# A fused attention and feed-forward block: the second entry's rows and the first splits turned by VectorE and HBM instead of TensorE

## The chip, the cores and the metric

The kernel runs on one core of a Trainium2 chip, in one launch. The time is device microseconds of one execution; lower is better. Five engines run side by side, each with its own queue in order: TensorE (PE, with its weight loads PEld), VectorE (DVE), ScalarE (ACT), GpSimd (POOL) and SyncE (SP), which issues all DMAs here. In the profile "L403" is line 403 of the kernel.

## The reference

Two entries of 1024 rows, 512 wide, in float32. Each layer is `x + layernorm(f(layernorm(x)))`: first causal attention with 16 heads of 128, then a gated feed-forward part whose weights are made ternary.

```python
x = x + _layernorm(_L0_attn_ref(_layernorm(x, axis=-1), W_Q, W_K, W_V, W_O), axis=-1)
x = x + _layernorm(_L0_ffn_ref(_layernorm(x, axis=-1), w1, w3, w2), axis=-1)

# attention, for each entry b and head h
q, k, v = (einsum('bsd,hed->bhse', x, W) for W in (W_Q, W_K, W_V))
scores = where(causal, -1e9, einsum('bhse,bhme->bhsm', q, k) / sqrt(128))
out = einsum('bhse,hde->bsd', einsum('bhsm,bhme->bhse', softmax(scores), v), W_O)

# feed-forward, 1365 hidden units; each w made ternary: clip(round(w / s), -1, 1) * s, s = mean(|w|)
out = einsum('bsh,dh->bsd', silu(x @ w1q.T) * (x @ w3q.T), w2q)
```

## The kernel before, in words

**Precision.** The products of the attention part take each float32 operand as three forms in fp32r: a leading one, a low one and their difference (`lead`, `low`, `diff`). The feed-forward part takes the rows as two (`hi`, `lo`), since ternary weights are exact.

**Rows as operands.** A projection needs the normalised rows turned, with the 512 columns on the partitions. One tile is 128 rows by 512 columns. For the first layer `block_unit(b, t)` turns tile t (0 to 7) of entry b: four TensorE transposes of 128x128 into PSUM, then ScalarE writes `lead`, VectorE `low`, GpSimd (or VectorE at the start) `diff`. The turned forms stand in tiles `xb`, of which there are six. For the second layer `split_units` gives three stages: `load` (the rows back from HBM, for entry 0), `normal`, and `split_turn` (four TensorE transposes, then `hi` and `lo`). Only the first split, of entry 0's first four tiles, runs that way. The twelve later ones, in the feed-forward stage, run through `split_stages`: VectorE transposes the tile in blocks of 32x32 (`xs`), one DMA writes it to HBM (`hopx`), four DMAs read it back with the blocks in place (`xu`), and then `hi` and `lo` are made from SBUF.

**Steps.** The attention stage is a loop over 32 (entry, head) pairs n and 8 query tiles i, 256 steps of some 4 to 7 us; `idx` counts them. In each step the source issues, in this order: weight loads; the step's `fill` (projections, output units, values), each on TensorE behind the newest matmul; forms of weights; the scores of three steps ahead (`look(idx + AHEAD)`); the rest of the values; the turning of the probabilities of two steps ahead (`turn`, which writes `blocks` to `hop` and later reads it back as `pt`); and last the step's `side` work. `tc.issue_after` (through `past` and `behind`) sets the order on an engine: the side work stands behind the last row maximum on VectorE, behind the last clearing of `blocks` on GpSimd, and behind the last turn on VectorE or SP. Within these bounds the compiler orders by its own plan. Loads, row statistics and the ternary weights are side work.

**The second entry's rows.** Its first projection stands in step 120. `block_at` is step 117. Tile t is loaded in the side work of step 114 + t, normalised by ScalarE (`normal_unit`, L388) in that of 115 + t, and turned in the fill of step 117 + t (`block_unit`, L403 to L409), with a PSUM buffer of the tag "mm" that the matmuls use as well. `split_at` is step 245: loads three steps ahead, normalisations two ahead (L123), turns in the fill of 245 + t (L256 to L259).

**Buffers.** PSUM holds four buffers "mm" and two "s_ps" for scores. In SBUF, `xt` has three buffers, `zf` (a copy of the values, read by VectorE's low form L667) two, `ones` is a constant for summing over partitions (L165).

**Start.** `busy(k)` issues k transposes of the identity that nobody reads. The first four tiles of entry 0 are turned in the buffers "s_ps".

Of the kernel before, what the change touches and what calls it, by code (L numbers as in the profile page):

```python
# [9 lines left out]
FP = mybir.dt.float32  # L10
# [9 lines left out]
FR = mybir.dt.float32r  # L20
T12 = 4096.0
LEAD = 1.0 - 0.5 / T12
# [13 lines left out]
def sandwich_kernel(  # L36
# [40 lines left out]
    )  # L77
    ones = const.tile([P, P], FP, name="ones")
    nc.gpsimd.memset(ones, 1.0)
    eps = const.tile([P, 1], FP, name="eps")  # L80
# [58 lines left out]
    def mean_abs_units(k, pool):  # L139
        todo = pieces(k)  # L140
        part = keep.tile([P, len(todo)], FP, name=f"part{k}")

        raws = {}

        def load(n):
            src, rows, cols = todo[n]
            raws[n] = raw = pool.tile([P, D], FP, name="xt")
            nc.sync.dma_start(raw[:rows, :cols], src)

        def reduce(n):  # L150
# [12 lines left out]
        def last():  # L163
            ps = ps_m.tile([P, 512], FP, name="tr", tag="mm")
            newest[0] = nc.tensor.matmul(  # L165
                ps[:, 0:1], lhsT=ones, rhs=raws["tot"], start=True, stop=True
            )
            for i, f in enumerate((0.5, -0.5, 1.0)):
                nc.vector.tensor_scalar(
                    scales[k][:, i : i + 1], ps[:, 0:1], 1.0 / (D * F), f,  # L170
                    ALU.mult, ALU.mult,
                )

        pairs = [
            (lambda n=n: load(n), lambda n=n: reduce(n)) for n in range(len(todo))
        ]
        return pairs, total, last
# [51 lines left out]
    def split_units(b, tb, t, stage):  # L229
# [13 lines left out]

        return load, normal, lambda: split_turn(b, tb, t, held["x"])

    def split_unit(b, tb, t, stage):
        for unit in split_units(b, tb, t, stage):
            unit()

    def split_turn(b, tb, t, xt):  # L250
        if t == 0:
            split[b, tb] = [xblocks.tile([P, NC, TB], FR, name="xb") for _ in range(2)]
        bl = split[b, tb]
        ps = ps_m.tile([P, NC, P], FP, name="trx", tag="mm")
        for c in range(NC):
            newest[0] = nc.tensor.transpose(ps[:, c, :], xt[:, ts(c, P)], ident)  # L256
        hi, lo = (part[:, :, ts(t, P)] for part in bl)
        nc.scalar.copy(hi, ps)
        nc.vector.tensor_tensor(lo, ps, hi, ALU.subtract)  # L259

# [77 lines left out]
    with ExitStack() as att:  # L338
# [39 lines left out]
        def block_load(b, t):  # L378
            normal[b, t] = xt = xpool.tile([P, D], FP, name="xt")
            nc.sync.dma_start(xt, x[b, ts(t, P), :])  # L380

        def normal_unit(b, t):
            if b == 0:
# [9 lines left out]
        def block_unit(b, t):  # L393
# [3 lines left out]
            xt = normal[b, t]  # L397
            if b == 0:
                ps = ps_s.tile([P, NC, P], FP, name="tr", tag="s_ps")
            else:  # L400
                ps = ps_m.tile([P, NC, P], FP, name="tr", tag="mm")
            for c in range(NC):
# [234 lines left out]
        def values(n, m):  # L637
# [21 lines left out]
            lead, low, diff = (w[:, ts(half, KB)] for w in zs[g, qb, j])  # L659
            copy = zpool.tile([P, KB], FP, name="zf", bufs=2)  # L660
            for to, scale in ((lead, LEAD / T12), (copy, 1.0)):
# [46 lines left out]
        with past(*done):  # L708
# [3 lines left out]
            for t in range(QT):  # L712
                blocks.append(block_unit(0, t))
                if t % 2 == 1:
                    busy((8, 3)[t // 2])
        lead, low, diff = blocks[-1]
# [32 lines left out]
        block_at = 2 * (NP - 1) * NT + 5  # L749
        assert at + 1 < block_at - 3  # L750
        for t in range(NT):
            side[block_at - 3 + t].append(lambda t=t: block_load(1, t))
            side[block_at - 2 + t].append(lambda t=t: normal_unit(1, t))
        at += (1 - at) % 4 + 4
# [16 lines left out]

        split_at = (N - 2) * NT + 5
        splits = [split_units(0, 0, t, xpool) for t in range(QT)]
        for t in range(QT):
            side[split_at - 3 + t].append(splits[t][0])
            side[split_at - 2 + t].append(splits[t][1])

# [35 lines left out]
        for n in range(N):  # L813
# [22 lines left out]
            if j == 0 and g > 0:  # L836
                outs = output_units(g - 1)
                put((0, 0, 0, 1, 4, 5, 6, 7), outs)
            for t in range(NT):
                if divmod(block_at + t, NT)[0] == n:  # L840
                    put([(block_at + t) % NT], [lambda t=t: block_unit(1, t)])
            for t in range(QT):
                if divmod(split_at + t, NT)[0] == n:
                    put([(split_at + t) % NT], splits[t][2:])
            if n == N - 1:
# [57 lines left out]
    with ExitStack() as ffn:  # L903
# [85 lines left out]

        def split_stages(b, tb, t):  # L990

            load, normal, _ = split_units(b, tb, t, xpool)
            if t == 0:
                split[b, tb] = [xblocks.tile([P, NC, TB], FR, name="xb") for _ in range(2)]
            held = {}

            def turn():
                xs = xpool.tile([P, 4, NC, 32], FP, name="xs", bufs=2)
                nc.vector.transpose(
                    xs.rearrange("p to c r -> p c to r"),  # L1000
                    normal().rearrange("p (b r) -> p b r", r=32),
                )
                held["d"] = d = dram.tile([P, 4, NC, 32], FP, name="hopx", bufs=2)
                nc.sync.dma_start(d, xs)

            def read():
                held["u"] = u = xpool.tile([P, 4, NC, 32], FP, name="xu", bufs=2)
                for to in range(4):
                    nc.sync.dma_start(
                        u[ts(to, 32)].rearrange("x a c r -> x a (c r)"),  # L1010
                        held["d"][:, to].rearrange("(a x) c r -> x a (c r)", a=4),
                    )

            def forms():
                u = held["u"]
                hi, lo = (
                    part[:, :, ts(t, P)].rearrange("p c (a r) -> p a c r", a=4)
                    for part in split[b, tb]
                )
                nc.scalar.copy(hi, u)  # L1020
                nc.vector.tensor_tensor(lo, u, hi, ALU.subtract)

            return load, turn, read, forms

        last = {}
# [91 lines left out]
```

## Time and profile before

| what | value |
|---|---|
| median of 3 runs | 1511.98 us (1511.87 to 1513.71) |
| profiled execution | 1511.27 us |
| its span | 1509.5 us |
| mean granted TensorE clock | 0.997 |
| TensorE transposes of the second entry's rows (L403, xt) | 32, from 592.2 to 627.9 us |
| TensorE transposes of the first splits (L256) | 16, from 1218.2 to 1229.4 us |
| VectorE transposes of the later splits (L999) | 12, median 711 ns |
| landing of hopx<-xs, of xu<-hopx | 2.1 us, 2.1 us (medians) |

The profile gives, for each engine, its busy time and the idle time before each group of instructions, with the instruction whose end released it ("<-DVE acc L530"). The profiled execution is one run; its span leaves out what comes before the first and after the last instruction. Matmuls overlap in the records: the time that one takes from TensorE is the distance to the next one's start. A group of the page with "+7 forms" mixes shapes.

### The profile page before, as it was taken

To read this page: it belongs to the slowest core of one execution; us is meant where nothing else is said; L and a number is where in the kernel's file an instruction comes from. 1 tells how busy PE (TensorE), PEld (TensorE's weight loads), DVE (VectorE), ACT (ScalarE), POOL (GpSimd) and SP (SyncE) were. 2 spreads that over 40 slices of the span, in tenths; PEclk is the share of its full clock that TensorE was granted. 3 is DMA by queue.
4 is the path that set the end of the run, shared out by engine and by line. 5 is a ranking of instruction groups with operands and counts; after the bars stand their busy time and mean duration, and the time that the engine had idled before them with its cause. 6 is when DMAs were issued, how large, how long until landed. Compare 5 with 4: busy or idle time off the path is not lost.

```text
span 1509.5 us, 21335 instructions
## 1 busy us (share of the span) xinstructions
PE 1475.6 (98%) x7061; PEld 1184.9 (78%) x7061; DVE 1080.6 (72%) x2123; ACT 792.7 (53%) x1566; POOL 404.3 (27%) x472
## 2 busy tenths in 40 slices
PE   8999999999999999999999999999999999999997
PEld 6778888887878787777778787878787877888885
DVE  7767686878786878787777777777777776664444
ACT  4656555555555555666664555555555464444332
POOL 3222222222223333434433333333322110210010
PEclk9999999999999999999999999999999999999999
DMA  3666767676666675758866666666665677530200
GB/s 123 194 194 186 195 184 200 185 202 184 201 191 172 181 206 183 205 166 249 238 200 190 195 192 196 195 195 189 179 179 166 181 216 228 176 102 19 91 28 29
DMA packets 179894, 263.57 MB, mean 175 GB/s; under 512 B 19188, under 2 KB 120564, under 8 KB 175688
## 3 DMA queue, kind: packets, MB, share of 16 engines
q1 hardware_dynamic: 179784, 262.20, 59.5%
q8 instruction: 57, 0.93, 0.3%
q14 instruction: 53, 0.43, 0.1%
HBM read 160.43 MB, written 101.71 MB: 174 GB/s over the span
## 4 chain that ended last, share of the span: by engine, by line
PE 66%; issue 10%; DVE 9%; DMA 7%; ACT 5%; POOL 2%; SPq 1%; DVEq 0%; POOLq 0%; ACTq 0%
PE mm L650 11%; PE mm L471 10%; PE mm L318 10%; PE s_ps L556 10%; PE mm L499 8%; PE mm L519 6%; PE yp L933 5%; PE mm L478 5%; DVE nm L565 3%; DMA hop<-blocks 2%; ACT p_sb L572 2%; DMA wqk<-wk 2%; ACT p_sb L578 1%; POOL kl L440 1%; DVE blocks L604 1%
## 5 line engine op out<-in xcount | busy, mean ns | idle before, releaser
L572 ACT ACTIVATE p_sb<-s_ps,nm 128x128 f32<-128x128 f32 (+7 forms) x256 | 190.0, 742 | 367.3 <-DVE nm L565 360.8
L556 PE MATMUL s_ps<-k,q 128*128 128x512 f32 (+3 forms) x768 | 289.7, 486 | 0.7 <-ACT p_sb L572 0.7
L650 PE MATMUL mm<-pt,v_sb 128*128 128x256 f32 (+1 forms) x1280 | 271.7, 359 | 11.3 <-ACT q L454 3.7
L650 PEld LDWEIGHTS mm<-pt,v_sb 128*128 128x128 f32 x1280 | 238.1, 190 | 48.8 <-ACT q L454 6.2
L578 ACT ACTIVATE p_sb<-p_sb,ri 128x128 f32<-128x128 f32 (+7 forms) x256 | 197.7, 773 | 33.0 <-DVE ri L577 30.5
L565 DVE TENSOR_REDUCE nm<-s_ps 128x1 f32<-128x128 f32 (+7 forms) x256 | 193.7, 757 | 7.1
L604 DVE STREAM_TRANSPOSE blocks<-p_sb 128x128 f32<-128x128 f32 (+7 forms) x256 | 197.1, 770 | 1.2 <-ACT p_sb L578 0.9
L556 PEld LDWEIGHTS s_ps<-k,q 128*128 128x128 f32 x768 | 132.3, 190 | 69.4 <-issue 61.4
L670 POOL TENSOR_TENSOR zd<-za,zl 128x256 fp32r<-128x256 f32 x128 | 94.7, 739 | 328.0 <-DVE zl L667 319.7
L561 DVE TENSOR_TENSOR s_ps<-s_ps,causal 128x128 f32<-128x128 f32 x256 | 75.4, 295 | 136.1 <-PE s_ps L556 135.6
L499 PE MATMUL mm<-va,xb 128*128 128x256 f32 x512 | 158.5, 310 | 0.0
L499 PE MATMUL mm<-vd,xb 128*128 128x256 f32 x512 | 144.9, 283 | 0.9 <-POOL xb L409 0.9
L499 PE MATMUL mm<-vl,xb 128*128 128x256 f32 x512 | 144.6, 282 | 0.0
L471 PE MATMUL mm<-xb,qa 128*128 128x512 f32 x256 | 119.6, 467 | 1.0 <-ACT xb L407 1.0
L471 PE MATMUL mm<-xb,ka 128*128 128x512 f32 x256 | 112.3, 439 | 0.0
L499 PEld LDWEIGHTS mm<-vl,xb 128*128 128x128 f32 x512 | 97.7, 191 | 7.1 <-issue 4.1
L499 PEld LDWEIGHTS mm<-va,xb 128*128 128x128 f32 x512 | 97.7, 191 | 7.1 <-issue 3.9
L471 PE MATMUL mm<-xb,ql 128*128 128x512 f32 x256 | 101.7, 397 | 0.0
L471 PE MATMUL mm<-xb,kl 128*128 128x512 f32 x256 | 100.7, 393 | 0.1
L499 PEld LDWEIGHTS mm<-vd,xb 128*128 128x128 f32 x512 | 97.7, 191 | 1.1 <-POOL xb L409 1.1
L601 POOL MEMSET blocks<- 128x128 f32 x128 | 26.2, 205 | 263.1 <-DMA hop<-blocks 185.2
L533 DVE TENSOR_TENSOR acc<-acc,mm 128x512 f32<-128x512 f32 x128 | 86.1, 683 | 12.7 <-ACT acc L528 5.4
(162 smaller groups left out, 2777.3 us busy)
## 6 DMA issues: line engine op xcount, KB each, us to landing
hop<-blocks SPq DMA_DIRECT2D x32, 1024.0 KB, 4.5
pt<-hop SPq DMA_DIRECT2D x128, 256.0 KB, 6.2
hop<-blocks SPq DMA_DIRECT2D x32, 768.0 KB, 3.3
pt<-hop SPq DMA_DIRECT2D x128, 192.0 KB, 3.8
hop<-blocks SPq DMA_DIRECT2D x32, 512.0 KB, 3.2
pt<-hop SPq DMA_DIRECT2D x128, 128.0 KB, 3.2
wqk<-wq SPq DMA_DIRECT2D x32, 256.0 KB, 5.2
wqk<-wk SPq DMA_DIRECT2D x32, 256.0 KB, 6.6
```

The costliest lines, as they stand in the source:

```text
L318: newest[0] = nc.tensor.matmul(ps[:fl, :], lhsT=t[:, c, :], rhs=bl[k][:, c, :], start=(c == 0 and k == 0), stop=(c == NC - 1 and k == 1),)
L471: newest[0] = nc.tensor.matmul(main, lhsT=forms[f][0][:, c, :], rhs=forms[f][1][:, c, :], start=(c == 0 and f == 0), stop=(c == NC - 1 and ...
L499: newest[0] = nc.tensor.matmul((main, main, diff)[f][:, ts(t, 2 * P)], lhsT=forms[f][0][:, c, token], rhs=forms[f][1][:, c, :], start=(t = ...
L519: newest[0] = nc.tensor.matmul((main, main, diff)[f], lhsT=zs[g, t // QT, j][f][:, ts(t % QT, P)], rhs=weights[3, g][f][:, 2 * j : 2 * j + ...
L533: nc.vector.tensor_tensor(dst, dst, diff, ALU.subtract)
L556: newest[0] = nc.tensor.matmul(s_ps[:, ds(k0, kl)], lhsT=proj[n, 0, i // QT][:, ts(i % QT, P)], rhs=proj[n, 1, k0 // TB][:, :kl], start=Tr ...
L565: top = nc.vector.tensor_reduce(nm, s_ps[:, :L], axis=AX.X, op=ALU.max, negate=True)
L572: e = nc.scalar.activation(p_sb[:, :L], s_ps[:, :L], AF.Exp, bias=nm, accum_out=rs)
L578: nc.scalar.mul(p_sb[:, :L], p_sb[:, :L], ri)
L604: turned = nc.vector.transpose(b[:, :, 0 : i + 1, il, :].rearrange("p to t r -> p t to r"), p_sb[:, :L].rearrange("p (b r) -> p b r", r=32),)
L650: newest[0] = nc.tensor.matmul(dst, lhsT=proj[g, 2][:, kt, ts(j, P)], rhs=rhs, start=(kt == 0), stop=(kt == 2 * m + 1),)
L670: nc.gpsimd.tensor_tensor(diff, lead, low, ALU.subtract)
```

## The change

The eight tiles of the second entry and the four of the first split are turned as the later splits are. `turn_stages` holds the two stages `turn` and `read`; `split_stages` moves out of the feed-forward part and uses it, with one buffer for `xs` there as well (two before), and two for `xu`. `block_stages(t)` gives five stages for tile t of the second entry, in the side work 6 (load), 5 (normalise), 4 (turn and write), 3 (read back) and 1 (forms) steps ahead of `block_at + t`. The low form of these is made by four VectorE instructions, one for each 128 columns. The first splits run 5 (load), 4 (normalise, turn and write), 3 (read back) and 1 (forms) steps ahead of `split_at + t`. To find room in SBUF, `zf` goes from two buffers to one, and the constant `ones` becomes a tile of the rotating `xt` that GpSimd sets when it is needed, three times. At the start, tiles 2 and 3 of entry 0 take buffers "mm" in place of "s_ps", and the unread transposes go from 8 and 3 to 7 and 8.

```diff
-    ones = const.tile([P, P], FP, name="ones")
-    nc.gpsimd.memset(ones, 1.0)
...
             ps = ps_m.tile([P, 512], FP, name="tr", tag="mm")
+            ones = pool.tile([P, D], FP, name="xt")
+            nc.gpsimd.memset(ones, 1.0)
             newest[0] = nc.tensor.matmul(
-                ps[:, 0:1], lhsT=ones, rhs=raws["tot"], start=True, stop=True
+                ps[:, 0:1], lhsT=ones[:, :P], rhs=raws["tot"], start=True, stop=True
             )
...
-    def split_turn(b, tb, t, xt):
-        if t == 0:
-            split[b, tb] = [xblocks.tile([P, NC, TB], FR, name="xb") for _ in range(2)]
-        bl = split[b, tb]
-        ps = ps_m.tile([P, NC, P], FP, name="trx", tag="mm")
-        for c in range(NC):
-            newest[0] = nc.tensor.transpose(ps[:, c, :], xt[:, ts(c, P)], ident)
-        hi, lo = (part[:, :, ts(t, P)] for part in bl)
-        nc.scalar.copy(hi, ps)
-        nc.vector.tensor_tensor(lo, ps, hi, ALU.subtract)
+    def turn_stages(pool):
+        held = {}
+
+        def turn(xt):
+            xs = pool.tile([P, 4, NC, 32], FP, name="xs", bufs=1)
+            nc.vector.transpose(
+                xs.rearrange("p to c x -> p c to x"), xt.rearrange("p (b r) -> p b r", r=32)
+            )
+            held["d"] = d = dram.tile([P, 4, NC, 32], FP, name="hopx", bufs=2)
+            nc.sync.dma_start(d, xs)
+
+        def read():
+            held["u"] = u = pool.tile([P, 4, NC, 32], FP, name="xu", bufs=2)
+            for to in range(4):
+                nc.sync.dma_start(
+                    u[ts(to, 32)].rearrange("r a c x -> r a (c x)"),
+                    held["d"][:, to].rearrange("(a r) c x -> r a (c x)", a=4),
+                )
+
+        return turn, read, held
+
+    def by_group(form, t):
+        return form[:, :, ts(t, P)].rearrange("p c (a x) -> p a c x", a=4)
+
+    def split_stages(b, tb, t, pool):
+        load, normal = split_units(b, tb, t, pool)
+        turn, read, held = turn_stages(pool)
+
+        def forms():
+            if t == 0:
+                split[b, tb] = [xblocks.tile([P, NC, TB], FR, name="xb") for _ in range(2)]
+            hi, lo = (by_group(part, t) for part in split[b, tb])
+            nc.scalar.copy(hi, held["u"])
+            nc.vector.tensor_tensor(lo, held["u"], hi, ALU.subtract)
+
+        return load, lambda: turn(normal()), read, forms
...
+        def block_stages(t):
+            turn, read, held = turn_stages(xpool)
+
+            def forms():
+                k, tl = divmod(t, QT)
+                if tl == 0:
+                    xs[1, k] = [xblocks.tile([P, NC, TB], FR, name="xb") for _ in range(3)]
+                lead, low, diff = (by_group(form, tl) for form in xs[1, k])
+                nc.scalar.mul(lead, held["u"], LEAD / T12)
+                for c in range(NC):
+                    nc.vector.scalar_tensor_tensor(
+                        low[:, :, c], lead[:, :, c], -T12, held["u"][:, :, c],
+                        ALU.mult, ALU.add,
+                    )
+                lead, low, diff = (form[:, :, ts(tl, P)] for form in xs[1, k])
+                nc.gpsimd.tensor_tensor(diff, lead, low, ALU.subtract)
+
+            return (
+                lambda: block_load(1, t), lambda: normal_unit(1, t),
+                lambda: turn(normal[1, t]), read, forms,
+            )
...
-            if b == 0:
+            if t in (2, 3):
+                ps = ps_m.tile([P, NC, P], FP, name="tr", tag="mm")
+            else:
                 ps = ps_s.tile([P, NC, P], FP, name="tr", tag="s_ps")
-            else:
-                ps = ps_m.tile([P, NC, P], FP, name="tr", tag="mm")
...
-            copy = zpool.tile([P, KB], FP, name="zf", bufs=2)
+            copy = zpool.tile([P, KB], FP, name="zf", bufs=1)
...
-                    busy((8, 3)[t // 2])
+                    busy((7, 8)[t // 2])
...
-        assert at + 1 < block_at - 3
+        assert at + 1 < block_at - 6
         for t in range(NT):
-            side[block_at - 3 + t].append(lambda t=t: block_load(1, t))
-            side[block_at - 2 + t].append(lambda t=t: normal_unit(1, t))
+            for stage, ahead in zip(block_stages(t), (6, 5, 4, 3, 1)):
+                side[block_at - ahead + t].append(stage)
...
-        splits = [split_units(0, 0, t, xpool) for t in range(QT)]
         for t in range(QT):
-            side[split_at - 3 + t].append(splits[t][0])
-            side[split_at - 2 + t].append(splits[t][1])
+            for stage, ahead in zip(split_stages(0, 0, t, xpool), (5, 4, 3, 1)):
+                side[split_at - ahead + t].append(stage)
...
-            for t in range(NT):
-                if divmod(block_at + t, NT)[0] == n:
-                    put([(block_at + t) % NT], [lambda t=t: block_unit(1, t)])
-            for t in range(QT):
-                if divmod(split_at + t, NT)[0] == n:
-                    put([(split_at + t) % NT], splits[t][2:])
...
-                stages = [split_stages(nb, ntb, t) for t in range(QT)]
+                stages = [split_stages(nb, ntb, t, xpool) for t in range(QT)]
```

More of the change, by code (lines that the diff above doesn't have):

```diff
@@ L242, in normal @@
             return held["x"]
[L244 to L248, printed above, removed]
-    def split_turn(b, tb, t, xt):
-        if t == 0:
-            split[b, tb] = [xblocks.tile([P, NC, TB], FR, name="xb") for _ in range(2)]
-        bl = split[b, tb]
-        ps = ps_m.tile([P, NC, P], FP, name="trx", tag="mm")
-        for c in range(NC):
-            newest[0] = nc.tensor.transpose(ps[:, c, :], xt[:, ts(c, P)], ident)
-        hi, lo = (part[:, :, ts(t, P)] for part in bl)
-        nc.scalar.copy(hi, ps)
-        nc.vector.tensor_tensor(lo, ps, hi, ALU.subtract)
+        return load, normal
+    def turn_stages(pool):
[27 more added lines that the diff above has]
+        return load, lambda: turn(normal()), read, forms
     def middle_units(b, pool):
@@ L988, in finish_last @@
                 nc.sync.dma_start(out[b, ts(tt, P), :], y)
[L990 to L1023, printed above, removed]
         last = {}
```

## The prediction

> **What bounds the kernel now.** I read the page first: who is busy, and what the chain of waits consists of.
>
> ```profile
> span 1509.5 us, 21335 instructions
> PE 1475.6 (98%) x7061; PEld 1184.9 (78%) x7061; DVE 1080.6 (72%) x2123; ACT 792.7 (53%) x1566; POOL 404.3 (27%) x472
> ...
> PE 66%; issue 10%; DVE 9%; DMA 7%; ACT 5%; POOL 2%; SPq 1%; DVEq 0%; POOLq 0%; ACTq 0%
> ```
>
> TensorE (PE) lacks work for only 33.9 us of the span, so the first question of any edit is how much TensorE time it removes, and the second is whether another engine then makes TensorE wait. Both are read from TensorE's timeline around the second entry's rows (t is the tile of 128 rows, 0 to 7).
>
> ```profile
> 590.54 1.78 PE L650 MATMUL mm<-pt,v_sb 128*128 128x256 f32 x8 [1.65 <-DVE acc L530]
> 592.16 0.60 PE L403 MATMUL tr<-ident,xt 128*128 128x128 f32 x4
> 592.59 0.39 PE L556 MATMUL s_ps<-k,q 128*128 128x128 f32 x2
> ...
> 609.65 0.39 PE L499 MATMUL mm<-vd,xb 128*128 128x256 f32 x1 [0.92 <-POOL xb L409]
> ...
> 612.38 0.66 PE L403 MATMUL tr<-ident,xt 128*128 128x128 f32 x4 [1.27 <-ACT xt L388]
> ...
> 614.42 0.65 PE L403 MATMUL tr<-ident,xt 128*128 128x128 f32 x4 [0.31 <-ACT xt L388]
> ```
>
> Four transposes show 0.60 us, but matmuls overlap: what counts is start to next start, 592.16 to 592.59, 0.43 us. The brackets are TensorE idle: 2.5 us of it (0.92, 1.27, 0.31) hang on rows or forms that come late, 1.65 on VectorE (DVE). So I asked for the busy time by stretch, each about one step of the schedule (columns: us, then PE, PEld, DVE, ACT, POOL busy, clock, DMA share, GB/s).
>
> ```profile
> 570.20:576.50 6.30, 6.30 (x29) 5.04 (x28) 3.52 (x9) 3.55 (x8) 1.96 (x3) 1.00 0.46 148
> 576.50:580.00 3.50, 3.50 (x16) 2.44 (x15) 3.11 (x8) 2.15 (x4) 3.16 (x4) 1.00 0.68 201
> 580.00:586.00 6.00, 6.00 (x25) 4.25 (x24) 5.73 (x10) 3.74 (x8) 2.70 (x3) 1.00 0.45 133
> 586.00:593.00 7.00, 5.35 (x28) 4.36 (x27) 5.74 (x10) 4.77 (x9) 0.21 (x1) 1.00 0.70 187
> 593.00:598.10 5.10, 5.10 (x26) 4.20 (x26) 4.75 (x10) 2.47 (x7) 2.20 (x2) 1.00 0.31 127
> 598.10:602.90 4.80, 4.80 (x26) 4.02 (x25) 3.38 (x10) 3.02 (x8) 2.81 (x4) 1.00 0.99 309
> 602.90:608.20 5.30, 5.30 (x41) 4.81 (x40) 2.92 (x8) 2.83 (x7) 3.48 (x3) 1.00 1.05 215
> ```
>
> VectorE is nearly full from 576.5 to 598 and has room before and after. The change puts new VectorE work into exactly these steps.
>
> **The change, part by part.** The sum is against the profiled execution, 1511.27 us (its span and 1.8 us around it), which is 0.7 below the median 1511.98; I add that back at the end.
>
> *TensorE transposes go.* Eight tiles at L403 and four at L256, 12 x 0.43 = 5.2 us, in stretches where TensorE is the bound. Their PSUM slots (tag "mm", shared with the matmuls) go too; I count nothing for that.
>
> *Stalls at those transposes go.* The forms are now finished in the side work of the step before the one in which the transposes stood, so the 0.92, 1.27 and 0.31 go: 2.5 us. What is late next is in the ledger below. At the first splits TensorE waits 0.69 us at 1232.04 (ACT p_sb L572, itself behind VectorE). There VectorE is 4.77 busy of 4.80 from 1220.1 to 1224.9; the earlier stages take two normalisations (L123, about 0.5 us each) out of these steps. I take 0.4 us.
>
> *Start.* Tiles 2 and 3 of the first entry get PSUM buffers of their own, so they no longer wait for VectorE to empty the first two.
>
> ```profile
> 8.90 0.81 ACT L388 ACTIVATE acc<-acc,shift,r_in 128x512 f32<-128x512 f32 x1 [0.43 <-DVE shift L371]
> ...
> 10.97 1.25 PE L403 MATMUL tr<-ident,acc 128*128 128x128 f32 x8 [1.83 <-DVE xb L408]
> ...
> 11.67 1.19 ACT L407 ACTIVATE xb<-tr 128x512 fp32r<-128x512 f32 x2 [0.98 <-PE tr L403]
> ```
>
> Rows 2 are normalised at 9.71, so ScalarE (ACT) can go on at 10.7 instead of 11.67, and VectorE's L408 at 11.5 instead of 12.31: 0.8 us earlier. From there the chain is VectorE's and GpSimd's (POOL), the latter not moved: I take 0.7 us, bounds 0 and 2. For the added filler transposes a rule stands against a row. TensorE: Matmul & The Clock Gate, Part 1, of the Trainium skill lets the clock fall to half after an idle window of about 3.4 us; here the longest gap is 1.83 us, so by the rule filler buys nothing. The row says the granted clock was 0.50 from 14 to 16 us after that gap. By the row a closed gap could save up to 2 us of TensorE time; but qd and kd come from VectorE at 17.57 and 19.26, so both give 0 here and the row only sets the far bound.
>
> *VectorE pays.* The nearest row for the new transpose is the same operation in the later stage, 128x512: 0.71 us (L999), and 0.62 from start to next start by L604's 512-wide one (571.73 to 572.35). Twelve of them, 7.4 us. The low form, one L408 of 0.60 start to start, becomes four pieces of 128 columns. No row has them; below, no more than 0.60 in all; above, four of L561's 0.295, 1.2. From L667's 256 columns (581.30 to 581.63, 0.33) I take 0.21 each, 0.85: 0.25 more per tile, 2 us for eight. The total is 9.4 us, more than the 5.2 that TensorE is spared; it is worth doing only where VectorE has room. Tile 0's turn falls into 2.79 us that VectorE spends waiting for POOL kl before 575.86: free. Before L530 at 589.80, which frees the slot that TensorE waits for at 590.54, come then tile 1's turn (0.62 less 0.32 idle), tile 2's and 3's (0.62 each) and tile 0's low form (0.85): 2.4 us, and the 1.65 stall grows to about 4. In the next two steps each gets 0.62 + 0.25 against 0.33 and 1.42 idle: 0.7 us reach TensorE. In the three steps after 603 there are over 2 us idle each: nothing. At the splits the turns fall into steps with 0.7 to 3.7 us idle: nothing.
>
> Here a rule speaks against the change: VectorE: DVE Perf Modes, Rules for kernel authors, says to transpose 128x128 on TensorE where a PSUM destination will do. By engine time it is right here too (0.43 against 0.71 a tile): 12 x 0.28 = 3.3 us slower, 1515.3. But it prices engines, not the bound: in the trace TensorE has no idle to give and VectorE has some, so I follow the trace.
>
> *The trip through HBM.* Per tile one write and four reads, five issues of about 0.43 us on SP's queue (2.1 us), 0.5 MB. SP stands mostly at L615, waiting for VectorE's blocks; its pt<-hop reads are needed about 9 us after landing, which covers 2 us of issue; past that L650 would wait. With xs at one buffer, a turn waits in VectorE's queue for the write of the tile before to land, and behind it stand L561 and L565, which ScalarE's exponentials and then TensorE wait for. Turns are 3.7 to 6.4 us apart (by L604's ends). In the later stage the write lands in 2.1 us, but here it follows hop<-blocks of up to 1 MB (4.5 us). Tile 5 follows tile 4 after 3.7 us: about 2 us of wait, part in the 1.42 idle: I take 0.8, bounds 0 and 4 for all. DMA share is about 1.0 from 598 to 608; loads move out of it, hops move in: 0.3, bounds -1 and 3. GpSimd contention with the low form, now SBUF only: L1021 has a median of 0.684 and a mean of 0.776, and one of 1.78; 8 x 0.1, of which 0.3 reach TensorE.
>
> *Counted at nothing.* ScalarE's normalisation (L388, 0.80 us) moves three steps ahead, its leading form one; both stay one step behind what they wait for, and ScalarE has 1.2 to 3 us idle a step. If a load lands later than a step, ScalarE waits with the exponentials behind it, as it does for 2.0 us in all now. GpSimd's difference form (1.29 us) moves a step ahead with 2 us idle or more in each. zf with one buffer: ScalarE's second copy must wait for VectorE's zl of the product before. Over 127 pairs the zl had ended 1.9 us or more ahead, but once 0.75; cover gone, ScalarE waits with the exponentials behind it, about as long as VectorE is late (2.4 us, once). The ones tile: a GpSimd memset three times, before L165; GpSimd has gaps of 1 to 3 us before each; without them TensorE waits one 1.3 us L440, 0 to 4 us in all. xs at one buffer in the last stage: turns 2.3 us apart at 1290.9 and 1293.2 could collide, covered by stages that run two steps ahead of their use.
>
> **Sum.** Gains 5.2 + 2.5 + 0.4 + 0.7 = 8.8. Costs 2.4 + 0.7 + 0.8 + 0.3 + 0.3 = 4.5. Net -4.3: 1507.0 beside the profiled run, 1507.7 beside the median.
>
> **Rivals.** *VectorE takes it all back.* If the transfer of work lands wholly where VectorE is full, its 9.4 us reach TensorE against gains of 8.8: 1512.6. For: DVE 5.74 busy in a step in which TensorE already waits. Against: half of the turns fall into steps with idle. *The single xs buffer holds VectorE's queue.* Ten turns follow another. If the write lands as the slowest xt<-x does here (8.2 us, in the stretch where DMA share is 1.0) instead of 2.1, each waits about 3 us: 30 us, less 11 idle in these steps and up to 7 that one step of lookahead covers (scores are issued three steps ahead into two buffers), some 12 on TensorE: 1519.5. It decides once these waits add 7.3 us on TensorE beyond my 0.8. For: DMA share 0.99 and 1.05. Against: most writes here land in 3 to 5 us. *It doesn't do what it says:* rows read back too late, so that matmuls wait for xb as at 609.65; two steps (10 us) lie between read and forms, so this is worth 2 us at most, 1509.7, counted with the even case. *All of VectorE's part is hidden:* 1503.2.
>
> **How the numbers follow.** 0.2% is 3.0 us, about what a measurement of this kernel can tell from no change: faster is below 1509.0, slower above 1515.0. The forecast with the hidden case 0.50, VectorE takes it back 0.25, the xs wait and other late transfers 0.25. The likeliest case alone is 1503 to 1510. The range reaches from 1502 (hidden, with 1 us more at the start) to 1518, leaving out the far part of the slow case.
>
> **What would show it.** L403 with xt and L256 gone; the stall near 590 grown to about 4 us and named after VectorE, no stall on xt or xb between 605 and 615; turns of 0.7 us without idle ended by DMA before them; the first L471 about 1 us earlier. Wrong if TensorE's idle between 560 and 640 exceeds 8 us, or VectorE idles on hopx.

## The result, and the profile after

| kernel | median us | runs | profiled execution, span |
|---|---|---|---|
| before | 1512.85 | 1511.87 to 1514.48 (4) | 1511.27, 1509.5 |
| after | 1526.15 | 1525.48 to 1531.38 (4) | 1525.56, 1523.8 |

The changed kernel takes 1.0094 times as long (95% interval 1.0069 to 1.0119; this ratio and the later ones are of means), 13.3 us more by the medians. I had forecast 4.3 us less. The page of the kernel after, the same lines as shown of before:

```profile
span 1523.8 us, 21439 instructions
PE 1479.1 (97%) x7017; PEld 1185.2 (78%) x7017; DVE 1095.8 (72%) x2159; ACT 792.5 (52%) x1566; POOL 404.6 (27%) x474
...
PE 62%; issue 10%; DVE 10%; DMA 8%; ACT 6%; POOL 2%; SPq 1%; DVEq 0%; POOLq 0%; ACTq 0%
```

TensorE has 44 instructions fewer and is nonetheless busy 3.5 us longer, and it lacks work for 44.7 us in place of 33.9. Of VectorE's 15.2 us more, 8.4 are the twelve added turns. To place the loss I number the score tiles by VectorE's masking of each (L561 before, L610 after: 256 of them, 0 to 255) and subtract their starts. The difference is -0.5 us at tile 0, -0.2 from tile 16 to tile 116, then rises to +10.3 by tile 129 (the second entry's rows), stays between 9.5 and 10.8 until tile 252, rises to +15.0 by tile 255 (the first splits), and is +14.3 at the first and at the last down projection (yp). So there are two losses, about 10.5 and 4.2 us, and none in the feed-forward stage.

TensorE's timeline at the rows (start, duration, instruction, in brackets the idle time before it and what ended it):

```profile
590.12 1.78 PE L699 MATMUL mm<-pt,v_sb 128*128 128x256 f32 x8 [1.41 <-ACT q L503]
...
600.52 4.30 PE L699 MATMUL mm<-pt,v_sb 128*128 128x256 f32 x12 [2.22 <-DMA pt<-hop]
...
611.90 0.38 PE L548 MATMUL mm<-va,xb 128*128 128x256 f32 x1 [1.27 <-ACT xb L417]
...
614.83 1.22 PE L548 MATMUL mm<-vd,xb 128*128 128x256 f32 x4 [0.96 <-POOL xb L424]
...
619.00 3.48 PE L699 MATMUL mm<-pt,v_sb 128*128 128x256 f32 x16 [0.97 <-DMA pt<-hop]
...
641.14 2.87 PE L699 MATMUL mm<-pt,v_sb 128*128 128x256 f32 x8 [4.47 <-DMA pt<-hop]
```

The stall near 590 did not grow (1.65 before). What is new is the wait for pt: probabilities that come back late from their own trip, whose code the change does not touch. The stretch table adds what such a wait costs afterwards (columns as in the prediction; the eighth number is the granted clock):

```profile
599.00:600.00 1.00, 0.00 (x0) 0.00 (x0) 1.00 (x4) 0.72 (x3) 0.00 (x0) 1.00 1.18 199
600.00:601.00 1.00, 0.48 (x2) 0.42 (x3) 1.00 (x5) 0.54 (x1) 0.00 (x0) 0.83 0.44 78
601.00:602.00 1.00, 1.00 (x4) 0.82 (x3) 1.00 (x5) 0.46 (x2) 0.42 (x1) 0.50 0.47 176
602.00:603.00 1.00, 1.00 (x4) 0.82 (x3) 0.49 (x3) 0.57 (x2) 0.85 (x1) 0.50 0.99 182
603.00:604.00 1.00, 1.00 (x4) 0.73 (x4) 1.00 (x4) 0.00 (x0) 0.00 (x0) 0.50 1.07 428
```

A gap of 2.22 us is followed by over 3 us at half clock. The means of the stretches 600 to 605, 610 to 615, 615 to 620 and 640 to 645 are 0.66, 0.93, 0.73 and 0.66, against 1.00 in all seven stretches shown of before. Five times the missing shares is 5.1 us at most. The 10.5 us then read: TensorE's idle time between 560 and 660 grew by 7.9 (4.15 to 12.02), the absent transposes are worth 3.4 by the prediction's price (eight tiles at 0.43), and some 6 remain, of which the clock explains 5.1 at most. About 1 us is placed nowhere.

Why pt comes late is seen in SP's queue. First before, then after:

```profile
582.67 0.34 SPq L615 DMA_DIRECT2D hop<-blocks  x1
583.05 1.39 SPq L380 DMA_DIRECT2D xt<-x  x2
586.86 1.75 SPq L631 DMA_DIRECT2D pt<-hop  x4
```

```profile
584.54 0.35 SPq L664 DMA_DIRECT2D hop<-blocks  x1
586.38 1.93 SPq L262 DMA_DIRECT2D xu<-hopx  x4
593.24 0.34 SPq L257 DMA_DIRECT2D hopx<-xs  x1
593.62 0.43 SPq L406 DMA_DIRECT2D xt<-x  x1
594.17 1.81 SPq L680 DMA_DIRECT2D pt<-hop  x4
```

From 588.3 to 593.2 SP stands at the write of hopx, because VectorE's turn of that tile (L253) runs only at 592.51. Behind it stands the read of pt. Its hop was issued at 584.54 and took 4.7 us to land, so the read could have started at about 589.2. It starts at 594.17, 7.3 us later than before: 5.0 by standing behind the write of hopx, the rest because its own hop landed later (586.8 before). TensorE waits for it until 600.52. Yet VectorE itself never waits for the trip; the groups of its turns show no idle ended by a DMA:

```profile
L253 DVE STREAM_TRANSPOSE xs<-xt 128x512 f32<-128x512 f32 x24 | 16.9, 704 | 0.2
```

So my first theory was that SP's single queue costs it: late turns, or simply five more issues per tile. The rivals: VectorE's added work, the bytes, the single buffer of xs, one of the small edits.

### The profile page after: what moved, and what is told of

Read it like the earlier page. It is cut to its first block, busy times and chain, and to the rows that moved or that the text cites. A ratio compares the mean times of both kernels' runs of the same rounds, so it can differ in the third digit from the quotient of the medians.

```text
span 1523.8 us, 21439 instructions
## 1 busy us (share of the span) xinstructions
PE 1479.1 (97%) x7017; PEld 1185.2 (78%) x7017; DVE 1095.8 (72%) x2159; ACT 792.5 (52%) x1566; POOL 404.6 (27%) x474
## 4 chain that ended last, share of the span: by engine, by line
PE 62%; issue 10%; DVE 10%; DMA 8%; ACT 6%; POOL 2%; SPq 1%; DVEq 0%; POOLq 0%; ACTq 0%
PE mm L699 10%; PE mm L344 10%; PE s_ps L605 9%; PE mm L520 9%; PE mm L548 8%; PE mm L568 6%; PE yp L975 5%; PE mm L527 4%; DMA hop<-blocks 3%; DVE nm L614 3%; ACT p_sb L621 3%; DMA wqk<-wk 2%; DMA pt<-hop 1%; POOL kl L489 1%; DVE blocks L653 1%
## 5 line engine op out<-in xcount | busy, mean ns | idle before, releaser
L610 DVE TENSOR_TENSOR s_ps<-s_ps,causal 128x128 f32<-128x128 f32 x256 | 75.4, 295 | 133.7 <-PE s_ps L605 133.1
```

## The experiments

All medians are beside runs of the kernel before on the same chip (1511.9 to 1512.6 in the five groups of runs).

**Which part of the change.** The three kernels put the rows, the splits, or both back on TensorE, exactly as in the diff's removed lines. rows_only keeps the rows' trip, splits_only that of the splits, rest_only neither.

```diff
 # splits_only and rest_only: rows on TensorE
-            for stage, ahead in zip(block_stages(t), (6, 5, 4, 3, 1)):
-                side[block_at - ahead + t].append(stage)
+            side[block_at - 3 + t].append(lambda t=t: block_load(1, t))
+            side[block_at - 2 + t].append(lambda t=t: normal_unit(1, t))
```

> The first splits go back to TensorE; the second entry's eight tiles stay with VectorE and HBM, and so do the edits at the start, to ones, zf and xs. Read from the two traces, the rows cost 10.5 us, the splits with what follows them 4.2, and the start gives 0.2. If these parts are independent, as the theory of SP's queue has it (each trip delays only the hop writes and pt reads near it): 1512.9 + 10.5 - 0.2 = 1523 us. If the last part of the slowdown is one that the rows cause and that only shows at the end, or that the edits to zf and ones cause, the time stays at 1526.

> The second entry's eight tiles go back to TensorE; the first splits stay with VectorE and HBM. Independent parts: 1512.9 + 4.2 - 0.2 = 1517 us. If the splits are only late because the whole schedule is displaced, or if zf and xs with one buffer are to blame, it is another number: 1513 in the first case, above 1520 in the second.

> Rows and splits both go back to TensorE; left are the start (tiles 2 and 3 in ps_m, more filler), ones in an xt slot, zf and xs with one buffer. The theory gives these 0.2 us of gain: 1512.5 to 1512.9. If zf with one buffer or the ones tile were behind part of the loss, it would be slower than before by 2 us or more. My prediction had 0.7 us of gain for the start.

| kernel | median us | ratio to before, interval |
|---|---|---|
| rows_only | 1522.16 | 1.0062 (1.0047 to 1.0077) |
| splits_only | 1516.36 | 1.0028 (1.0020 to 1.0037) |
| rest_only | 1512.27 | 0.9997 (0.9988 to 1.0005) |

The parts add up: 9.9 and 4.1 us on top of rest_only, together 14.0, against 13.9 measured for the whole. The edits to zf, ones, the start and the feed-forward stage are worth nothing measurable, so the start's 0.7 us of my sum is not there either.

**Another queue.** In the attention stage the trip is issued from another engine: all of it from GpSimd (q_pool), only the write from ScalarE (q_act_write), all of it from ScalarE (q_act).

```diff
-            nc.sync.dma_start(d, xs)
+            nc.gpsimd.dma_start(d, xs)   # q_act_write, q_act: nc.scalar
...
-                nc.sync.dma_start(
+                nc.gpsimd.dma_start(     # q_act: nc.scalar; q_act_write: nc.sync
                     u[ts(to, 32)].rearrange("r a c x -> r a (c x)"),
```

> The changed kernel, with the write of hopx and the reads of xu in the attention stage issued from GpSimd's queue in place of SP's; VectorE's work, xs, zf and all bytes are as in the changed kernel. Theory of SP's queue: hop writes and pt reads no longer stand behind a write that waits for a late turn, the waits of TensorE for pt near 600, 619 and 641 (2.2, 1.0 and 4.5 us) and the lowered clock behind them go, as does most of the 4.2 us at the splits: 1510 to 1516 us, unless GpSimd's own forms are held up by the issues. Theory that VectorE's 9.4 us of added work, or one buffer of xs, is the cause: nothing moves, 1524 to 1528. Theory of DMA bandwidth: the same, 1524 to 1528.

> The changed kernel, with only the write of hopx in the attention stage issued from ScalarE's queue; the four reads of xu stay with SP, and hopx stays on the hardware queues. GpSimd's queue gave 1540.7: the waits for pt were gone there, but ScalarE, VectorE and GpSimd then stood at hopx and xu. Theory of SP's queue, in the form that SP stands still at a hopx write whose turn is late: hop writes and pt reads regain their places except for 1.8 us of reads, and the 7.7 us of idle named after pt mostly go: 1515 to 1521. Rival, that the issue time of the five DMAs fills SP: no better than 1524. If ScalarE now stands at the late turn with the exponentials behind it, it is slower than 1526.

> As the run before, with the reads of xu on ScalarE's queue too. SP is then as in the kernel before. If SP's order is all that counts: 1510 to 1516. If ScalarE stands at the landing of hopx (it did so for 22 us with GpSimd's queue, by way of xu), the exponentials wait for it: 1525 or more. Each trip also takes 2.1 us of ScalarE's time.

Measured: 1540.73, 1533.72 and 1534.81 us (ratios 1.0185, 1.0136 and 1.0149, each within 0.0016). All three are slower than the change, against every number of my theory. What came true are the branches in which ScalarE waits in SP's place: over 1526 for q_act_write, 1525 or more for q_act. In q_pool and q_act TensorE no longer waits for pt between 560 and 660, as the theory had it, but the wait came back elsewhere. In q_act_write, where only the write has left SP, 4.9 of the 7.7 us of waiting for pt remain. The waits of q_pool between 560 and 660 (us in total, times, longest), first TensorE's, then ScalarE's:

```profile
PE mm L549 <- POOL xb L425: 9.3, 1, 9.3
PE mm L700 <- ACT q L504: 6.8, 1, 6.8
```

```profile
ACT xb L418 <- DMA xu<-hopx: 21.9, 6, 7.4
```

GpSimd now stands at hopx with its own difference forms behind, and ScalarE at xu with the exponentials behind. q_pool and q_act bear out that pt was late by what stood ahead of it on SP, but none of the three shows a cure.

**VectorE's work or the DMAs, with dummies.** TensorE turns all rows as before (rest_only). dve_extra adds VectorE's eight turns of a constant tile without DMA. dma_extra adds the eight writes and 32 reads without turns. The next three vary dma_extra: tiny DMAs, the same bytes in two DMAs, reads that need not wait for the write.

```diff
+        def extra_turn(t):        # side work at block_at - 4 + t
+            xs_ = xpool.tile([P, 4, NC, 32], FP, name="xs", bufs=1)      # dve_extra
+            nc.vector.transpose(xs_.rearrange(...), dz.rearrange(...))
...
+            nc.sync.dma_start(d, dz.rearrange("p (a c x) -> p a c x", a=4, c=NC))  # dma_extra
+        def extra_read(t):        # side work at block_at - 3 + t
+            for to in range(4): ...                     # dma_extra: as xu<-hopx
```

> TensorE turns all rows, as in the kernel before; VectorE turns a constant tile of 128x512 into xs besides, in the eight steps in which the changed kernel has its turns (ahead 4), and nothing reads it. No DMA is added. It adds 8 x 0.71 us to VectorE and nothing else. Rival of VectorE's load: about 5 us on top of 1512.3, 1517. Theory of SP's queue: SP does not wait for these turns, so only what VectorE hands on directly: 1512.5 to 1514.5 (my prediction's working had 1.9 us for the turns alone).

> TensorE turns all rows, as in the kernel before; the eight writes of hopx and the 32 reads of xu are added from a constant tile in the same steps of the changed kernel, on SP's queue, and nothing reads xu. No VectorE work is added, and no write waits for a turn. It adds 17 us of issue to SP and 4 MB. If issue time or DMA bandwidth alone is the cause: about 10 us on top of 1512.3, 1522. If it is the standing of SP at writes that wait for late turns: 1513 to 1516.

> As dma_extra (five more DMAs per tile on SP's queue, from a constant tile, TensorE turns all rows), but each DMA moves 16 packets of 128 bytes in place of 256 and 64 KB. The number of issues and their places in SP's order are the same, the bytes are gone. dma_extra stood at 1521.8 beside 1512.3. If what costs is the time in which SP issues and the order in its queue: 1518 to 1522. If it is what the DMA engines have to move: 1512 to 1514.

> As dma_extra, with the same bytes in two DMAs per tile: one write of 256 KB and one read of 256 KB in rows of 2 KB, in place of one write and four reads of 512-byte pieces. SP issues 0.9 us per tile in place of 2.1. If issue time costs: 1513 to 1516. If bytes cost: 1518 to 1522. If the 512-byte pieces are what makes the bytes dear, it also falls to 1513 to 1516; issue_tiny then tells the two apart.

> As dma_extra, with the four reads per tile taken from x in place of hopx, in the same pieces of 512 bytes. So no read waits in SP's queue until a write has landed; issues and bytes are the same. If SP's standing at the landing of hopx (3.5 us in the trace of dma_extra between 570 and 650) moves the rest: 1513 to 1516. If not: 1520 to 1522.

| kernel | median us | ratio to before, interval |
|---|---|---|
| dve_extra | 1512.56 | 1.0006 (0.9997 to 1.0014) |
| dma_extra | 1521.76 | 1.0068 (1.0050 to 1.0085) |
| issue_tiny | 1515.08 | 1.0019 (1.0012 to 1.0026) |
| bytes_two | 1514.41 | 1.0011 (1.0002 to 1.0020) |
| dma_nowait | 1523.22 | 1.0068 (1.0053 to 1.0083) |

Eight turns more on VectorE cost nothing that can be measured: that rival falls. The DMAs alone cost 9.6 us, just the size that was looked for, which looked like an answer: not the issues (2.5), not the bytes (1.9), not the wait for the write's landing (dma_nowait is no better), but issues and bytes together. But TensorE's waits in dma_extra between 560 and 660 are others than in the changed kernel:

```profile
PE tr L463 <- ACT xt L448: 9.8, 5, 2.9
```

Here the rows are still loaded three steps ahead, and TensorE waits for their normalisation (L448). ScalarE shows no idle time ended by a load ahead of it, so the delay is in what ScalarE does first; it was not followed further. In the change the rows are loaded six steps ahead and nobody waits for them; it is pt that is late. A dummy whose loss has the right size and another wait proves nothing for the case. Why issues and bytes together cost more than their sum, the four issues or the 512-byte pieces of the reads, stays open.

**The trip inside the change.** So the next four keep rows_only's own turns and forms and vary only the trip. trip_none reads the forms from xs and makes no trip; trip_two makes it in two DMAs in natural layout; trip_tiny issues all five DMAs with 2 KB each; trip_real makes the real trip, back into the buffer that it left from. All have xs with three buffers and no xu for the rows.

```diff
-            xs = pool.tile([P, 4, NC, 32], FP, name="xs", bufs=1)
+            held["u"] = u = pool.tile([P, 4, NC, 32], FP, name="xs", bufs=3)
...
-            held["u"] = u = pool.tile([P, 4, NC, 32], FP, name="xu", bufs=2)
             for to in range(4):     # trip_real; trip_none leaves the DMAs out
```

> As rows_only (1522.2), with the trip left out for the second entry's rows: VectorE turns each tile into xs (three buffers), the forms are taken from xs three steps later, nothing is written to or read from HBM, so the blocks of 32 are not moved between partitions. VectorE's, ScalarE's and GpSimd's work is that of the change. By the sum of my prediction for the rows alone (3.4 of transposes, 2.5 of stalls, less 3.1 of VectorE and 0.3 of GpSimd): 1512.3 - 2.5 = 1509.8. If VectorE's work is free, as dve_extra showed for the turns: 1506.5 to 1508. If VectorE's low form in four pieces or the order of the forms is to blame: 1515 or more.

> As trip_none, with one write of 256 KB to hopx and one read of 256 KB back into the same buffer in rows of 2 KB, in the steps of the changed kernel: the trip's bytes and both of its waits, in two issues in place of five. Left out: the move of blocks between partitions. If bytes alone cost as with the dummies: trip_none + 2 us. If the bytes or the waits for the turns are the main cost: trip_none + 8 or more.

> As trip_none, with one write and four reads of 16 packets of 128 bytes each on SP's queue; the write waits for VectorE's turn as in the changed kernel, the reads for the write's landing. All of the trip's issues and waits in SP's order, none of its bytes. If issues and waits alone cost as with the dummies: trip_none + 2.5 to 4 us. If SP's standing at late turns is the main cost, as my first theory had it: trip_none + 8 or more.

> As rows_only, with xs and xu made one buffer of which there are three: the trip reads back into the buffer that it wrote from. All five issues and all bytes, and the result is the reference's. A turn no longer waits for the write of the tile before, but for the forms of the tile three before. If the single buffer of xs costs nothing: 1520 to 1523. If it is behind the loss: below 1516.

| kernel | median us | ratio to before, interval |
|---|---|---|
| trip_none | 1509.81 | 0.9985 (0.9979 to 0.9992) |
| trip_two | 1510.89 | 0.9989 (0.9983 to 0.9996) |
| trip_tiny | 1509.17 | 0.9977 (0.9969 to 0.9986) |
| trip_real | 1513.16 | 1.0007 (0.9996 to 1.0018) |

With three buffers, the issues with their waits (trip_tiny) and the bytes (trip_two) cost at most 1.1 us by the medians. The real trip costs 3.4 us more than none, no longer 12.4. What took 9.0 us off rows_only is the change of buffers, although nothing waited on xs visibly. If the single buffer cost nothing, as my theory had it, trip_real would have taken 1520 to 1523: the theory fell. The difference is in VectorE's timeline, first rows_only (third turn at 592.35), then trip_real (at 583.61); its other instructions between are left out:

```profile
580.25 0.70 DVE L264 STREAM_TRANSPOSE xs<-xt 128x512 f32<-128x512 f32 x1
...
586.58 0.29 DVE L621 TENSOR_TENSOR s_ps<-s_ps,causal 128x128 f32<-128x128 f32 x1
592.35 0.70 DVE L264 STREAM_TRANSPOSE xs<-xt 128x512 f32<-128x512 f32 x1
```

```profile
580.37 0.29 DVE L639 TENSOR_TENSOR s_ps<-s_ps,causal 128x128 f32<-128x128 f32 x1
583.61 0.69 DVE L265 STREAM_TRANSPOSE xs<-xt 128x512 f32<-128x512 f32 x1
586.64 0.28 DVE L639 TENSOR_TENSOR s_ps<-s_ps,causal 128x128 f32<-128x128 f32 x1
```

The turn has moved past a score tile. Counted by the score tiles ahead of them, the eight turns of the changed kernel and of rows_only stand behind tiles 116, 117, 119, 121, 121, 123, 124, 125; those of trip_real behind 116, 117, 118, 120, 121, 122, 123, 124. SP's order is the same in both. The compiler orders each engine by its own plan within the source's bounds, and here it gave the turns later places with one buffer. The wait is thus in the order, not in idle time: VectorE does other work first, and SP stands at the write.

One buffer does not always give late places. In q_pool, with one buffer too, the turns stand behind tiles 116, 117, 118, 119, 120, 121, 122, 124, and there VectorE does wait for the write, as the prediction had it (between 560 and 660):

```profile
DVE xs L254 <- DMA hopx<-xs: 5.7, 3, 4.4
```

Why the plan chose one form of the wait here and the other there, no run shows.

**Putting it back.** trip_gate is trip_real with a single-buffered tile of one number per partition, set ahead of each turn and read by a small DMA behind the write. trip_late asks whether the rest can be had by writing one step after the turn.

```diff
 # trip_gate
+                g = pool.tile([P, 1], FP, name="gate", bufs=1)
+                first = nc.vector.memset(g, 0.0)      # the turn is ordered behind it
...
                 nc.sync.dma_start(d, u)
+                nc.sync.dma_start(e[:16], g[:16])
 # trip_late: turn, write, read, forms
-            (6, 5, 4, 3, 1)
+            (6, 5, 4, 3, 2, 1)
```

> As trip_real (1513.2: xs and xu one tile with three buffers), with a tile of one number per partition and one buffer that VectorE sets ahead of each turn and that a DMA of 64 bytes behind the write of hopx reads: each turn again has to wait until the DMAs of the tile before have landed, as with one buffer of xs; xu's part is untouched. It adds 0.4 us of SP issue per tile. If the single buffer of xs and the later places it gives to the turns (after score tiles 116, 117, 119, 121, 121, 123, 124, 125 again) are the cause: 1519 to 1524. If xu's buffers were: 1513 to 1515.

> As trip_real, with the write of hopx one step later than its turn and the reads one step later too (turn four ahead, write three, reads two, forms one). SP then issues a write whose turn is done, behind the hop write of its own step. If what is left in trip_real beside trip_none (1513.2 against 1509.8) is SP standing at turns: 1509 to 1511.5, faster than before. If the bytes and the issues are what is left, or if the rows now come late for their forms: 1512 to 1515.

trip_gate: 1524.07 us (1.0081, 1.0065 to 1.0096), and its turns stand behind tiles 116, 117, 119, 121, 121, 123, 124, 125, as in the changed kernel. TensorE's largest wait in it between 560 and 660:

```profile
PE mm L733 <- DMA pt<-hop: 8.5, 2, 5.3
```

It has 0.4 us of SP issue per tile more than trip_real, but in trip_tiny five issues per tile, all small, cost nothing beside trip_none. So the loss at the rows comes from the single buffer: taking it away won 9.0 us, putting a like one back cost 10.9, and the places of the turns went with it. A gate with three buffers, which would part its own DMA from the wait, was not run. The way from the late turn over SP and pt to TensorE is read from the traces.

trip_late: 1523.26 us (1.0072, 1.0060 to 1.0085), a miss. Its waits for pt are gone, but with one step between read and forms the rows come late:

```profile
PE mm L581 <- ACT xb L450: 3.6, 2, 2.7
PE mm L553 <- DVE xb L452: 2.3, 1, 2.3
PE mm L553 <- ACT xb L450: 2.3, 1, 2.3
```

That is my prediction's rival "rows read back too late", which I had at 2 us at most for two steps between read and forms. A fourth buffer, with which all stages could keep two steps before the forms, was not tried. No version that does the whole work beats the kernel before; trip_none, trip_two and trip_tiny do, but leave the move of blocks between partitions out.

**The splits.** TensorE's timeline before shows one short wait at the first splits:

```profile
1232.04 0.49 PE L556 MATMUL s_ps<-k,q 128*128 128x128 f32 x2 [0.69 <-ACT p_sb L572]
```

In splits_only TensorE's timeline and then ScalarE's and VectorE's show the second loss:

```profile
1232.14 0.49 PE L605 MATMUL s_ps<-k,q 128*128 128x128 f32 x2 [1.91 <-ACT p_sb L621]
1233.91 0.74 PE L344 MATMUL mm<-xb,va 128*128 128x512 f32 x2 [1.29 <-ACT xb L282]
1235.73 4.94 PE L344 MATMUL mm<-xb,va 128*128 128x512 f32 x14 [1.08 <-DVE xb L283]
```

```profile
1232.31 1.04 ACT L627 ACTIVATE p_sb<-p_sb,ri 128x896 f32<-128x896 f32 x1 [0.23 <-DVE ri L626]
1233.26 0.60 ACT L282 CAST xb<-xu 128x512 fp32r<-128x512 f32 x1
```

```profile
1232.87 1.21 DVE L614 TENSOR_REDUCE nm<-s_ps 128x1 f32<-128x1024 f32 x1
1234.00 1.10 DVE L653 STREAM_TRANSPOSE blocks<-p_sb 128x896 f32<-128x896 f32 x1
1235.03 0.65 DVE L283 TENSOR_TENSOR xb<-xu,xb 128x512 fp32r<-128x512 f32 x1
```

The transposes had filled time in which TensorE would have waited for VectorE and ScalarE anyway (0.69 us on p_sb before, 1.91 now), and the last tile's forms stand behind the widest score work. The clock falls here too: its mean from 1226 to 1240 is 0.88 in splits_only and 1.00 before, which is 1.7 us of TensorE's time.

```diff
 # splits_early: splits_only with the stages a step earlier
-            for stage, ahead in zip(split_stages(0, 0, t, xpool), (5, 4, 3, 1)):
+            for stage, ahead in zip(split_stages(0, 0, t, xpool), (6, 5, 4, 2)):
```

> As splits_only (1516.4), with the stages of the first splits at six, five, four and two steps ahead in place of five, four, three and one. In splits_only the forms of tile 3 stand on ScalarE behind an L627 and on VectorE behind the 1024-wide L614 and the 896-wide L653, and TensorE waits 1.29 and 1.08 us for them at 1233.9 and 1235.7. If that place in the two engines' order costs the 4.2 us: 1511.5 to 1513. If the splits cost by SP's queue or by VectorE's work: 1515 to 1518.

Measured: 1514.61 us (1.0015, 1.0008 to 1.0022). The waits for xb are gone and half of the loss with them; about 2 us over the kernel before remain, and TensorE's wait for pt between 1200 and 1285 is 5.5 us where rest_only has 2.3. That the remainder has the same cause as at the rows was not tried.

## Why the prediction was wrong, by its steps

**The step that failed: xs at one buffer, 0.8 us, bounds 0 and 4.** It cost about 9 (rows_only less trip_real 9.0; trip_gate less trip_real 10.9). I looked for VectorE idle until the write lands, and the rival of 1519.5 did so too: right part, wrong form. The wait took the form of a later place for the turn, and the late turn was paid by SP, pt and TensorE. My mark for being wrong, VectorE idle on hopx, would have missed it; the other one, TensorE idle over 8 us between 560 and 640, held.

**SP's queue, 2.1 us of issue that 9 us of lead would cover.** I counted issue time and not standing. For SP's own part this was nearly right (trip_tiny costs nothing beside trip_none). Where a write stands 5 us at a turn, and the hop of pt lands later besides, the lead is gone.

**VectorE pays, 2.4 + 0.7.** The durations were right: turns 0.704 us, four pieces of the low form 0.85 (593.14), once 2.92 for eight (629.10, with a GpSimd difference form of 1.38 us running beside them). The cost was not: the stall near 590 fell to 1.41, and dve_extra shows the turns free. The rival "VectorE takes it back" is refuted for the turns. The rule that I set aside (the Trainium skill, VectorE: DVE Perf Modes, Rules for kernel authors: transpose 128x128 on TensorE where a PSUM destination will do) had given 1515.3. It had the right sign, but not by the engine time that I priced it with: in dve_extra that is free.

**Stalls go, 2.5.** Those on xt went, but 1.27, 0.29 and 0.96 on the forms xb took their place, 2.5 again. In trip_none idle between 560 and 660 is 4.36 against 4.15. So trip_none's 1509.81, which is the sum for the rows to the digit, is luck: no stall is gone, the turns cost nothing on VectorE, and after a gap of 2.43 us the clock stands at 0.50 from 611 to 613, which the sum has no term for.

**The transposes, 5.2.** For the rows the 3.4 was not seen whole: trip_none is 2.4 below before, 1.2 to 3.2 by the interval. For the splits nothing did: the step took TensorE for the bound there, and it was the score chain; 0.4 of gain was a loss of 4.1.

**The start, 0.7, and the clock.** The gap at 10.97 closed and the clock stayed at 1.00 from 14 to 20 us, but VectorE's qd and kd bind as the prediction says of them, and new gaps stand before them:

```profile
17.25 1.16 PE L527 MATMUL mm<-xb,qd 128*128 128x512 f32 x4 [1.03 <-DVE qd L495]
18.85 1.20 PE L527 MATMUL mm<-xb,kd 128*128 128x512 f32 x4 [0.44 <-DVE kd L495]
```

At the first score tile 0.5 us is gained, 0.2 at tile 16, nothing measurable in rest_only. As for the rule weighed there, of the Trainium skill (TensorE: Matmul & The Clock Gate, Part 1: half clock after an idle window of about 3.4 us), the row wins again: at 600 the clock fell after 2.22 us of gap, and at 614 after gaps of 1.27, 0.29 and 0.96. But the length of a gap does not settle it: a gap of 2.23 us at 600.38 in rows_only left the clock at 1.00. By the rule only the gap of 4.47 would have cost clock, and some 3.4 of the 5.1 us would be missing from the account. My sum had no term for the clock behind a new stall.

**Counted at nothing.** zf, ones and the later stage's xs are free indeed (rest_only; equal differences at first and last yp).

## What to carry to other kernels

When a change gives a tile fewer buffers, the wait need not show as idle time: count where the instruction stands in its engine's order, against a steady mark such as the score tiles, and ask who stands in a DMA queue behind its write. Price a trip by leaving it out inside the changed kernel (trip_none shows about what can be won, here 2.4 us), and trust a dummy only if it brings the same wait as well as the same loss. A stall of 2 us or more can cost TensorE 1.7 us again in clock: each of the three falls at the rows did.

## What the runs showed of the hardware

The clock stood at 0.50 by 601, half a microsecond after a gap of 2.22 us ended, and stayed there for some 3 us of full work. Whether such a gap costs clock varies. This one, of rows_only, left it at 1.00:

```profile
600.38 2.62 PE L710 MATMUL mm<-pt,v_sb 128*128 128x256 f32 x12 [2.23 <-DMA pt<-hop]
```

In the twenty traces, from 20 to 1500 us, TensorE has 29 gaps of 2.0 to 2.7 us; 12 of them left the clock at 1.00 over the next 5 us (the longest 2.66, at 612.60 in trip_tiny). All 16 gaps of 2.93 us and more were followed by 0.50. What decides in between is not shown.

Four reads of xu took 3.83 us to issue at 611.37, at a DMA share of 1.06, but 1.74 at 596.14, at a share of 1.00: a full share alone does not make SP's issue slow. Issued from GpSimd, the eight writes of hopx at the rows landed after 3.5 us (median, q_pool), from SP after 2.6 (the changed kernel), each in one profiled execution and among other transfers.
